# A layernorm's root on 128 columns, two products at a time, and a later front part

## The chip, the cores and the metric

The kernel runs on one core of a Trainium2 chip. Five engines work side by side, each through its own queue of instructions in order: TensorE (PE, matmuls; its weight loads are listed as PEld), VectorE (DVE), ScalarE (ACT), GpSimd (POOL, which here mostly starts DMAs) and SyncE (SP, which starts the other DMAs). The metric is the device time of one execution in microseconds (us), lower is better.

## The reference

The input is 8 images of 256 channels on 32 x 32 places, so 8 batches of 1024 tokens. Two layers follow each other. The first is a state-space block and a small two-layer network, the second is attention and a mixture of experts:

```python
xn = layernorm(x)                                  # over the 256 channels
xm, z = split(xn @ W_in)                           # 512 channels each
xm = silu(conv4(xm) + conv_b)                      # 4 taps along the tokens
dt, Bm, Cm = split(xm @ W_x, [16, 32])             # 16 + 16 + 16 columns
dt = softplus(dt @ W_dt + b_dt)                    # 16 -> 512
h = exp(dt * A) * h + (dt * xm) * Bm               # 16 states for each of 512 channels, in token order
y = (sum over states of h * Cm) + xm * D
x = x + (y * silu(z)) @ W_out
x = x + gelu(layernorm(x) @ W1 + b1) @ W2 + b2
t = x + attention(layernorm(x))                    # 8 heads, 1024 tokens, a bias for each key
xf = layernorm(t)
out = t + layernorm(xf + two chosen experts(xf)) * gamma + beta
```

There are five layernorms over 256 channels on each token: `a` before the state-space block, `f` before the small network, `t` before attention, `x` before the experts, `y` at the end.

## The kernel before

**Tiling.** Channels lie on the 128 partitions, tokens along the free dimension, in chunks of 512 tokens: two chunks for each batch, 16 in all. A 256-channel activation of a chunk is one tile of 128 x 2 x 512 floats. Everything is float32, and a float32 matmul shows as two records in the trace.

**The steps of the scan.** The main loop goes over 16 chunks x 32 steps (`nsteps` = 512). A step is one state of one half of the 512 channels: `inputs` (a product `hb<-xm,bc` on DVE), two calls of `scan` (each a TENSOR_TENSOR_SCAN of 128 x 512 on DVE, fed by an exponential `da` from ACT, made by `decay` two steps ahead), `sums` (a product `hb<-hb,bc` on DVE), after which a DMA that POOL starts adds `hb` into the sum `dx`. In the first chunk of a batch POOL also copies the last column (`state`). bc is loaded two states ahead (`AHEAD`).

**The streams around it.** All other work is written as generators: `prologue(i)` (the front part of chunk i: layernorm, input projection, convolution, dt), `gate_part(i)`, `epilogue(i)` (output projection, small network, layernorm `t`), `attention(b)`, `project_part`, `experts(b)`, `finish`. A planner at build time gives each operation a cost, keeps a planned time for each engine and, between two DVE operations of the scan, takes from each stream what its plan says is ready (`advance`). The order thus written is fixed: on the chip each engine runs its queue in that order and waits where an operand is not there yet. Where the plan finds PE without work it puts in a filler matmul (`keep_warm`: tile `warm`, or zeros added to an open sum of attention).

**What starts when.** `prologue(i + 1)` is started at step `FRONT` = 2 of chunk i, the gate part at step `GATE` = 17, `epilogue(i)` after the last step of chunk i. From step 30 on the scan of a chunk needs the next chunk's `dt`; when the front part has not given it, the planner calls `idle`: DVE gets no scan work there, while the other streams go on. Attention of a batch starts when both epilogues of the batch are done; experts when both chunks of attention are projected.

**Layernorm.** `layernorm` takes the mean by two matmuls with a constant 1/256 matrix (`mu`, 128 x 512), subtracts (DVE), squares (ACT), takes the variance by two such matmuls (`var`, 128 x 512: all 128 rows hold the same numbers), then 1/sqrt by ACT (`Ln`, `Exp`, `Square`, each 128 x 512) and one Newton step on DVE (two operations of 128 x 512), and a last DVE operation scales the tile: one of 128 x 1024, or for `x` and `y` two of 128 x 512. There are 16 of each kind, 80 in all.

**dt.** In the front part, `dbl` (48 rows: 16 for dt, 16 for B, 16 for C) is copied out of PSUM by ACT, one DMA stores the B and C rows (`bc_d`), and four matmuls with 16 rows of `w_dt` give dt for 128 channels each (tile `v`), each in a PSUM bank of its own, read by two ACT operations (`Abs`, `Relu`) before the next is asked for. Softplus goes on with ACT, one DVE operation (`e<-u,e`) and two adding DMAs started by POOL (`dt<-e`, `dt<-u`); the last operation is `xm<-xm,dt` on DVE for each half.

**PSUM.** Eight banks: two single banks (`banks`), two pairs (`pairs`, four banks, attention's scores), and two for attention's sums. A stream may borrow a half of a pair where no bank is free.

Nearly all records carry the line of a recording helper (L100, DMAs started by POOL or SP L95), so the views are read by tile names.

Of the kernel before, what the change touches and what calls it, by code (L numbers as in the profile page):

```python
# [9 lines left out]
F32 = mybir.dt.float32  # L10
BF16 = mybir.dt.bfloat16
I32 = mybir.dt.int32
AF = mybir.ActivationFunctionType
# [41 lines left out]
def hybrid_kernel(ctx: ExitStack, tc: tile.TileContext, a: dict, out: bass.AP):  # L55
# [85 lines left out]
    w_in = load("w_in", [P, KC, 2 * DI], a["W_in"].rearrange("(k p) n -> p k n", p=P))  # L141
    w_x = load("w_x", [P, ND, RK + 2 * NS], a["W_x"].rearrange("(k p) n -> p k n", p=P))
    w_dt = load("w_dt", [RK, DI], a["W_dt"])
    w_out = load("w_out", [P, ND, C], a["W_out"].rearrange("(k p) n -> p k n", p=P))
# [18 lines left out]

    ident = const.tile([P, P], F32, name="ident")
    make_identity(nc, ident)
    mean_c = const.tile([P, 1], F32, name="mean_c")
# [3 lines left out]
    pool.memset(zero_c, 0.0)  # L170
    zero_w = zero_c.to_broadcast([P, P])
    eps_t = const.tile([P, 1], F32, name="eps_t")
    pool.memset(eps_t, EPS)
# [3 lines left out]
    qscale = 1.0 / math.sqrt(HD)  # L177
    neg_a = const.tile([P, ND * NS], F32, name="neg_a")
    act.activation(neg_a, V("A_log"), AF.Exp)
    vec.tensor_scalar(neg_a, neg_a, -1.0, None, ALU.mult)  # L180
# [33 lines left out]
    base2 = const.tile([P, NF], F32, name="base2")  # L214
    gamma2 = const.tile([P, KC], F32, name="gamma2")

# [29 lines left out]
    T4, H4, PT, AHEAD, LAG, TICK = 25, 4, 4, 2, 8.0, 0.15  # L246
    FRONT, GATE = 2, 17

# [62 lines left out]
    class Banks(Slots):  # L311


        lent, halves = {}, []

        def take(self, name):
            while not self.ready() and not (len(pairs.free) == 2 and pairs.ready()):
                yield POLL
            if self.ready():
                return self.now(name)  # L320
            pair = pairs.now(name)
            ps = pair[:, 0, :]
            self.lent[id(ps)] = (ps, pair)
            return ps

        def put(self, ps):
# [41 lines left out]
    def layernorm(tmp, bank, src, dst, name, gain=None, bias=None, sums=None, stored=None):  # L368
# [17 lines left out]
        yield  # L386
        var = yield from bank.take(f"var_{name}")
        for k in range(KC):
            pe.matmul(var, mean_w, sq[:, k, :], start=(k == 0), stop=(k == KC - 1))
        yield  # L390

        r, h = sq[:, 0, :], sq[:, 1, :]
        act.activation(r, var, AF.Ln, bias=eps_t)
# [3 lines left out]
        vec.scalar_tensor_tensor(h, var, EPS, h, ALU.add, ALU.mult)  # L397
        bank.put(var)
        vec.scalar_tensor_tensor(r, h, -3.0, r, ALU.add, ALU.mult)
        if gain is None and sums is None:  # L400
            vec.scalar_tensor_tensor(
                dst, dst, -0.5, r.unsqueeze(1).to_broadcast([P, KC, CH]), ALU.mult, ALU.mult
            )
        else:
            for k in range(KC):
                vec.scalar_tensor_tensor(
                    dst[:, k, :], dst[:, k, :], -0.5 if gain is None else gain[:, k : k + 1], r,
                    ALU.mult, ALU.mult, accum_out=None if sums is None else sums[:, k, :],
                )
                if bias is not None:  # L410
                    vec.tensor_scalar(
                        dst[:, k, :], dst[:, k, :], bias[:, k : k + 1], None, ALU.add
                    )
        tmp.put(sq)
        return dst
# [23 lines left out]
    def prologue(i: int):  # L439
# [52 lines left out]
        for d in range(ND):  # L492
            pe.matmul(
                ps[: RK + 2 * NS, :], w_x[:, d, :], xm[d // 2][:, d % 2, :],
                start=(d == 0), stop=(d == ND - 1),
            )
        yield
        dbl = work_pool.tile([P, KW - 1 + CH], F32, name=f"dbl_{i}", tag="xp", bufs=2)
        dbl = dbl[: RK + 2 * NS, :CH]
        act.copy(dbl, ps[: RK + 2 * NS, :])  # L500
        banks.put(ps)
# [10 lines left out]

        for d in range(ND):
            h, q = divmod(d, 2)
            if q == 0:
                e = yield from mem.take(f"e_{i}_{h}")
                dts.append((yield from mem.take(f"dt_{i}_{h}")))
            ps = yield from banks.take(f"v_{i}_{d}")
            pe.matmul(ps, w_dt[:, d * P : (d + 1) * P], dbl[:RK, :], start=True, stop=True)
            if d == 0:  # L520
                bc_d = dram.tile([NS, 2, CH], F32, name=f"bc_d_{i}", tag="bc_d", bufs=3)
                sp.dma_start(bc_d.rearrange("s g t -> g s t"), dbl[RK:, :])
                me["bc_d"] = bc_d
            yield
            act.activation(e[:, q, :], ps, AF.Abs, bias=V("b_dt", d))
            act.activation(dts[h][:, q, :], ps, AF.Relu, bias=V("b_dt", d))
            banks.put(ps)
            if q == 0:
                continue
            u = yield from mem.take(f"u_{i}_{h}")  # L530
# [218 lines left out]
    def column_bias(pl):  # L749
# [3 lines left out]

        tr = pl.tmp("tr", [P, 4, P], I32)
# [196 lines left out]
    def expert_constants(pl):  # L953
        vec.memset(loads_e, 0.0)
        vec.tensor_scalar(gamma2, V("gamma"), -0.5, None, ALU.mult)
        for dst, n, step, mul, add in (
# [434 lines left out]
    def finish_last(b, c, r, r2, t, xf):  # L1391
# [17 lines left out]
    def finish(b: int, c: int, r, y):  # L1409
# [4 lines left out]
        yield pool.dma_start(out=r, in_=xf_d[b][c], accum_op=ALU.add)  # L1414
        yield from layernorm(mem, banks, r, r, f"y{b}_{c}", gamma2)
        yield
# [9 lines left out]

    def attention_any(pl, b: int):

# [75 lines left out]
    with tc.tile_pool(name="work", bufs=1) as work_pool:  # L1504
# [11 lines left out]
        class Scratch:  # L1516
# [155 lines left out]
    with tc.If(large != 0):  # L1672
        with tc.tile_pool(name="general", bufs=1) as pl:
            wqg = pl.tile([P, KC, NPAIR, P], F32, name="wqg")
            nc.sync.dma_start(wqg, a["Wq"].rearrange("(k p) (j n) -> p k j n", p=P, n=P))
# [14 lines left out]
            for b in range(B):  # L1690
                attention_any(pl, b)


        with tc.tile_pool(name="moe", bufs=1) as pl:
            io = pl.tile([P, E], F32, name="io_e")
            io_i = pl.tile([P, E], I32, name="io_ei")
# [97 lines left out]
            for b in range(B):  # L1794
# [33 lines left out]
                for c in range(NCH):  # L1828
# [13 lines left out]
                    for m in range(KC):  # L1842
# [13 lines left out]
                        r, res,  # L1856
                        f"m{n}", gamma2, V("beta"),
                    ))
# [63 lines left out]
```

## Time and profile before

| | |
|---|---|
| time before, median of 3 runs | 3675.86 us (3664.82, 3675.86, 3676.42) |
| the profiled execution | 3671.49 us, span 3669.6 us |
| mean granted clock of TensorE | 0.953 |
| PE busy (fillers too) | 3313.7 us, 90% |
| DVE busy | 3111.7 us, 85% |
| ACT busy | 2515.7 us, 69% |
| POOL busy | 950.3 us, 26% |
| HBM read and written | 234.36 MB and 58.20 MB, 80 GB/s |
| first scan starts, last scan ends | 92.3 us, 3226.8 us |

How to read the lines: in the page's second part a digit is the busy share of one of 40 equal slices of the span, in tenths. In the stretches each row is a window of the span, then for each engine its busy time and the number of its records. In the groups each row is an engine, an operation, out<-in by tile names, the shape, the count | busy time of all, mean duration of one in ns | idle time of the engine just before them, and what ended it. A matmul's shape begins with rows*columns of the array that it uses. In the timeline a row is start, duration, engine, operation, and in brackets the idle time of the engine just before.

### The profile page before, as it was taken

What the parts mean: (1) busy time and instruction counts of PE and PEld (TensorE: products, weight loads), DVE (VectorE), ACT (ScalarE), POOL (GpSimd) and SP (SyncE); (2) the same over time, 40 slices, a digit from 0 to 9 for tenths busy, and PEclk for the clock granted to TensorE, in tenths of its full rate; (3) what the DMA queues carried; (4) which work ended last, traced back from release to release, by engine and by line L of the source; (5) the groups of instructions that cost most, each with busy time, mean ns of one, the idle gap of its engine ahead of it and who ended that gap; (6) DMA issues with size and microseconds to landing.
All of it is one profiled execution on the core that took longest, in us unless ns stands there. A gap on an engine that the chain in (4) does not pass through costs nothing. (4 is left out here: it accounts for less than half of the span.)

```text
span 3669.6 us, 37029 instructions
## 1 busy us (share of the span) xinstructions
PE 3313.7 (90%) x13023; PEld 1404.1 (38%) x13023; DVE 3111.7 (85%) x3323; ACT 2515.7 (69%) x3437; POOL 950.3 (26%) x1047
## 2 busy tenths in 40 slices
PE   8866869998999998999899999989999989999997
PEld 5553434233343334333433334332433334334333
DVE  5979999999999999999999799999999999942121
ACT  3443746795868776878678877878578876764644
POOL 0323123212431224222322233222423233201010
PEclk9877989999999999999999999999999999999999
DMA  3457777787788778797878877897879887842130
GB/s 110 111 112 177 173 169 167 173 187 180 181 188 189 178 163 197 170 206 180 199 174 193 191 187 171 199 202 160 198 172 201 195 194 181 195 96 69 30 79 14
DMA packets 178868, 597.08 MB, mean 163 GB/s; under 512 B 25184, under 2 KB 27872, under 8 KB 178672
## 3 DMA queue, kind: packets, MB, share of 16 engines
q0 software_dynamic: 103392, 364.44, 50.9%
q1 hardware_dynamic: 75280, 230.18, 19.5%
q8 instruction: 104, 1.70, 0.2%
q14 instruction: 92, 0.75, 0.1%
HBM read 234.36 MB, written 58.20 MB: 80 GB/s over the span
## 5 line engine op out<-in xcount | busy, mean ns | idle before, releaser
L100 ACT ACTIVATE da<-dt,neg_a 128x512 f32<-128x512 f32 x1024 | 718.6, 718 | 525.7 <-DVE hb L100 506.0
L95 POOL DMA_DIRECT2D dx<-hb x512 | 444.2, 868 | 1671.0 <-DVE hb L100 1407.1
L100 DVE TENSOR_TENSOR hb<-hb,bc 128x1024 f32<-128x1024 f32 x512 | 624.5, 1220 | 39.3 <-POOL state L100 25.6
L100 DVE TENSOR_TENSOR_SCAN hb<-da,state,hb 128x512 f32<-128x512 f32 x512 | 631.1, 1267 | 6.0 <-ACT da L100 6.0
L100 DVE TENSOR_TENSOR hb<-xm,bc 128x1024 f32<-128x1024 f32 x512 | 615.9, 1203 | 10.1 <-DMA dx<-hb 10.1
L100 DVE TENSOR_TENSOR_SCAN hb<-da,hb 128x512 f32<-128x512 f32 x512 | 601.9, 1209 | 5.2 <-ACT da L100 5.1
L100 ACT ACTIVATE pt<-sc 128x1024 f32<-128x1024 f32 x512 | 493.5, 1016 | 71.5 <-PE sc L100 68.4
L100 PE MATMUL warm<-mean_c,zero_c 128*128 128x256 f32 x1568 | 440.5, 413 | 46.5 <-DVE x L100 6.5
L100 PEld LDWEIGHTS warm<-mean_c,zero_c 128*128 128x128 f32 x1568 | 293.7, 200 | 216.0 <-PE warm L100 73.9
L100 PE MATMUL sc<-qk,qk 32*128 32x512 f32 x2048 | 337.3, 642 | 19.1 <-ACT pt L100 15.7
L100 POOL COPY state<-hb 128x2 f32<-128x2 f32 x256 | 236.1, 922 | 424.1 <-DVE hb L100 407.7
L100 PE MATMUL num<-pt,v 128*32 128x512 f32 x2048 | 280.9, 618 | 25.1 <-DVE ot L100 24.4
L100 PE MATMUL den<-pt,ecb 128*32 128x512 f32 x2048 | 274.9, 606 | 0.0
L100 PE MATMUL facc<-fh,w 128*128 128x512 f32 x512 | 240.5, 621 | 18.5 <-ACT dt L100 5.9
L100 PE MATMUL fh<-x_f,w 128*128 128x512 f32 x480 | 229.6, 609 | 6.1 <-DVE x_f L100 2.3
L100 ACT ACT_TABLE_LOAD x171 | 219.4, 1283 | 8.5 <-PE var_a L100 4.9
L100 PE MATMUL he<-xe,g 128*128 128x512 f32 x448 | 220.9, 618 | 2.4 <-ACT he L100 2.1
L100 PE MATMUL re<-he,g 128*128 128x512 f32 x472 | 213.9, 598 | 1.2 <-ACT fh L100 0.6
L100 PEld LDWEIGHTS sc<-qk,qk 32*128 32x128 f32 x2048 | 99.3, 183 | 221.5 <-ACT pt L100 86.7
L100 PE MATMUL mo<-sz,w_out 128*128 128x512 f32 x256 | 129.0, 650 | 59.9 <-DVE sz L100 57.1
L100 PEld LDWEIGHTS facc<-fh,w 128*128 128x128 f32 x512 | 98.9, 198 | 152.9 <-issue 125.9
L100 DVE SCALAR_TENSOR_TENSOR xm<-xp,vecs,xm 128x512 f32<-128x512 f32 x192 | 143.4, 747 | 13.5 <-ACT xm L100 9.0
(328 smaller groups left out, 4231.7 us busy)
## 6 DMA issues: line engine op xcount, KB each, us to landing
dx<-hb POOLq DMA_DIRECT2D x512, 512.0 KB
bc<-bc_d SPq DMA_DIRECT2D x256, 512.0 KB
dt<-e POOLq DMA_DIRECT2D x32, 512.0 KB
dt<-u POOLq DMA_DIRECT2D x32, 512.0 KB
xe<-xf_d SPq DMA_DIRECT2D x28, 512.0 KB
xn<-in_x SPq DMA_DIRECT2D x16, 512.0 KB
xn_d<-xn SPq DMA_DIRECT2D x16, 512.0 KB
xz<-xn_d SPq DMA_DIRECT2D x16, 512.0 KB
```

What stands on the lines that cost most here:

```text
L95: f(*args, **kw)
L100: return f(*args, **kw)
```

## The change

Three things are changed, and small ones that follow from them.

1. **dt's products in pairs.** `w_x` has its 16 dt columns twice, in the order dt, B, dt, C, so `dbl` has 64 rows and the dt rows lie at rows 0 to 15 and 32 to 47. `w_dt` is laid out to match. The four matmuls become two pairs; the two of a pair read different rows of the array and write two banks, which are taken together (`take_two`: two single banks, or a whole pair). The four ACT operations on a pair follow together. The B and C rows are stored by two DMAs, since they are no longer neighbours.
2. **Narrow roots.** The variance matmuls write a quarter of the tokens each into 32 rows: eight matmuls (2 halves of the channels x 4 quarters) of 32 columns of the array and 128 tokens, instead of two of 128 x 512. `Ln`, `Exp`, `Square` and the Newton step then work on 128 x 128. Four matmuls with a column of `pick` (zeros, and -0.5 in the first row of a group of 32) spread the four quarters again over all 128 partitions, into the bank that held the variance, and the last DVE operation takes its factor from there. The factor -0.5 is now in `pick`.
3. **`FRONT` = 8**: `prologue(i + 1)` starts at step 8 of chunk i.

The identity matrix for transposes is no longer a constant tile but is made where it is used: in the setup stream, in one of now 9 slots that it borrows, and in the branch for rare inputs, which these inputs don't take. `neg_a` overwrites `A_log` in place, and `gamma2` is gone.

```diff
@@ -139,8 +139,16 @@
     work = ctx.enter_context(ExitStack())
     work.enter_context(tc.manual_schedule(engines=set(ENGINES)))
     w_in = load("w_in", [P, KC, 2 * DI], a["W_in"].rearrange("(k p) n -> p k n", p=P))
-    w_x = load("w_x", [P, ND, RK + 2 * NS], a["W_x"].rearrange("(k p) n -> p k n", p=P))
-    w_dt = load("w_dt", [RK, DI], a["W_dt"])
+
+    w_x = const.tile([P, ND, 4 * RK], F32, name="w_x")
+    w_dt = const.tile([3 * RK, NHALF, P], F32, name="w_dt")
+    wx_v = a["W_x"].rearrange("(k p) n -> p k n", p=P)
+    wdt_v = a["W_dt"].rearrange("r (h q n) -> q r h n", q=2, n=P)
+    loads += [
+        (w_x[:, :, : 2 * RK], wx_v[:, :, : 2 * RK]), (w_x[:, :, 2 * RK : 3 * RK], wx_v[:, :, :RK]),
+        (w_x[:, :, 3 * RK :], wx_v[:, :, 2 * RK :]),
+        (w_dt[:RK], wdt_v[0]), (w_dt[2 * RK :], wdt_v[1]),
+    ]
     w_out = load("w_out", [P, ND, C], a["W_out"].rearrange("(k p) n -> p k n", p=P))
     w1 = load("w1", [P, KC, HID], a["W1"].rearrange("(k p) n -> p k n", p=P))
     w2 = load("w2", [P, HID // P, C], a["W2"].rearrange("(k p) n -> p k n", p=P))
...
@@ -161,22 +169,24 @@
     be = load("be", [P, NH], a["be"].partition_broadcast(P))
     br_p = load("br", [P, E], a["br"].partition_broadcast(P))
 
-    ident = const.tile([P, P], F32, name="ident")
-    make_identity(nc, ident)
     mean_c = const.tile([P, 1], F32, name="mean_c")
     pool.memset(mean_c, 1.0 / C)
     mean_w = mean_c.to_broadcast([P, P])
     zero_c = const.tile([P, 1], F32, name="zero_c")
     pool.memset(zero_c, 0.0)
     zero_w = zero_c.to_broadcast([P, P])
+    pick = const.tile([P, 4], F32, name="pick")
+    pool.memset(pick, 0.0)
+    for q in range(4):
+        pool.memset(pick[HD * q : HD * q + 1, q : q + 1], -0.5)
     eps_t = const.tile([P, 1], F32, name="eps_t")
     pool.memset(eps_t, EPS)
 
 
 
     qscale = 1.0 / math.sqrt(HD)
-    neg_a = const.tile([P, ND * NS], F32, name="neg_a")
-    act.activation(neg_a, V("A_log"), AF.Exp)
+    neg_a = V("A_log")
+    act.activation(neg_a, neg_a, AF.Exp)
     vec.tensor_scalar(neg_a, neg_a, -1.0, None, ALU.mult)
     bq4 = const.tile([P, NG], F32, name="bq4")
     bk4 = const.tile([P, NG], F32, name="bk4")
...
@@ -244,7 +253,7 @@
 
 
     T4, H4, PT, AHEAD, LAG, TICK = 25, 4, 4, 2, 8.0, 0.15
-    FRONT, GATE = 2, 17
+    FRONT, GATE = 8, 17
...
@@ -311,7 +320,7 @@
     class Banks(Slots):
 
 
-        lent, halves = {}, []
+        lent, twos, halves = {}, {}, []
 
         def take(self, name):
             while not self.ready() and not (len(pairs.free) == 2 and pairs.ready()):
...
@@ -323,6 +332,24 @@
             self.lent[id(ps)] = (ps, pair)
             return ps
 
+        def take_two(self, name):
+
+            while True:
+                if len(self.free) > 1 and sorted(self.free)[1][0] <= model.t + 0.3:
+                    return [self.now(f"{name}_{n}") for n in range(2)]
+                if len(pairs.free) == 2 and pairs.ready():
+                    pair = pairs.now(name)
+                    self.twos[id(pair)] = pair
+                    return pair[:, 0, :], pair[:, 1, :], pair
+                yield POLL
+
+        def put_two(self, both):
+            if len(both) == 3:
+                pairs.put(self.twos.pop(id(both[2])))
+            else:
+                for ps in both:
+                    super().put(ps)
+
         def put(self, ps):
             if id(ps) in self.lent:
                 pairs.put(self.lent.pop(id(ps))[1])
...
@@ -384,33 +411,45 @@
             sq = src
         act.activation(sq, dst, AF.Square)
         yield
-        var = yield from bank.take(f"var_{name}")
+
+        ps = yield from bank.take(f"var_{name}")
+        var = ps[:, :P]
         for k in range(KC):
-            pe.matmul(var, mean_w, sq[:, k, :], start=(k == 0), stop=(k == KC - 1))
-        yield
-
-        r, h = sq[:, 0, :], sq[:, 1, :]
+            for q in range(4):
+                pe.matmul(
+                    var[HD * q : HD * q + HD, :], mean_w[:, :HD], sq[:, k, q * P : q * P + P],
+                    start=(k == 0), stop=(k == KC - 1),
+                )
+        yield
+
+        r, h = sq[:, 0, :P], sq[:, 1, :P]
         act.activation(r, var, AF.Ln, bias=eps_t)
         act.activation(r, r, AF.Exp, scale=-0.5)
         act.activation(h, r, AF.Square)
         yield
         vec.scalar_tensor_tensor(h, var, EPS, h, ALU.add, ALU.mult)
-        bank.put(var)
         vec.scalar_tensor_tensor(r, h, -3.0, r, ALU.add, ALU.mult)
+        yield
+
+        for q in range(4):
+            pe.matmul(
+                ps[:, q * P : q * P + P], pick[:, q : q + 1].to_broadcast([P, P]), r,
+                start=True, stop=True,
+            )
+        yield
         if gain is None and sums is None:
-            vec.scalar_tensor_tensor(
-                dst, dst, -0.5, r.unsqueeze(1).to_broadcast([P, KC, CH]), ALU.mult, ALU.mult
-            )
+            vec.tensor_tensor(dst, dst, ps.unsqueeze(1).to_broadcast([P, KC, CH]), ALU.mult)
         else:
             for k in range(KC):
                 vec.scalar_tensor_tensor(
-                    dst[:, k, :], dst[:, k, :], -0.5 if gain is None else gain[:, k : k + 1], r,
+                    dst[:, k, :], dst[:, k, :], 1.0 if gain is None else gain[:, k : k + 1], ps,
                     ALU.mult, ALU.mult, accum_out=None if sums is None else sums[:, k, :],
                 )
                 if bias is not None:
                     vec.tensor_scalar(
                         dst[:, k, :], dst[:, k, :], bias[:, k : k + 1], None, ALU.add
                     )
+        bank.put(ps)
         tmp.put(sq)
         return dst
...
@@ -491,13 +530,13 @@
         ps = yield from banks.take(f"dbl_{i}")
         for d in range(ND):
             pe.matmul(
-                ps[: RK + 2 * NS, :], w_x[:, d, :], xm[d // 2][:, d % 2, :],
+                ps[: 4 * RK, :], w_x[:, d, :], xm[d // 2][:, d % 2, :],
                 start=(d == 0), stop=(d == ND - 1),
             )
         yield
         dbl = work_pool.tile([P, KW - 1 + CH], F32, name=f"dbl_{i}", tag="xp", bufs=2)
-        dbl = dbl[: RK + 2 * NS, :CH]
-        act.copy(dbl, ps[: RK + 2 * NS, :])
+        dbl = dbl[: 4 * RK, :CH]
+        act.copy(dbl, ps[: 4 * RK, :])
         banks.put(ps)
         yield
...
@@ -510,23 +549,25 @@
             landed[h] = pool.dma_start(out=dts[h], in_=t, accum_op=ALU.add)
             mem.put(t, at=landed[h])
 
-        for d in range(ND):
-            h, q = divmod(d, 2)
-            if q == 0:
-                e = yield from mem.take(f"e_{i}_{h}")
-                dts.append((yield from mem.take(f"dt_{i}_{h}")))
-            ps = yield from banks.take(f"v_{i}_{d}")
-            pe.matmul(ps, w_dt[:, d * P : (d + 1) * P], dbl[:RK, :], start=True, stop=True)
-            if d == 0:
+        for h in range(NHALF):
+            e = yield from mem.take(f"e_{i}_{h}")
+            dts.append((yield from mem.take(f"dt_{i}_{h}")))
+            both = yield from banks.take_two(f"v_{i}_{h}")
+            for q, ps in enumerate(both[:2]):
+                rows = slice(2 * RK * q, 2 * RK * q + RK)
+                pe.matmul(ps, w_dt[rows, h, :], dbl[rows, :], start=True, stop=True)
+            if h == 0:
                 bc_d = dram.tile([NS, 2, CH], F32, name=f"bc_d_{i}", tag="bc_d", bufs=3)
-                sp.dma_start(bc_d.rearrange("s g t -> g s t"), dbl[RK:, :])
+                for g in range(2):
+                    rows = slice((2 * g + 1) * RK, (2 * g + 2) * RK)
+                    sp.dma_start(bc_d[:, g, :], dbl[rows, :])
                 me["bc_d"] = bc_d
             yield
-            act.activation(e[:, q, :], ps, AF.Abs, bias=V("b_dt", d))
-            act.activation(dts[h][:, q, :], ps, AF.Relu, bias=V("b_dt", d))
-            banks.put(ps)
-            if q == 0:
-                continue
+            for q, ps in enumerate(both[:2]):
+                d = 2 * h + q
+                act.activation(e[:, q, :], ps, AF.Abs, bias=V("b_dt", d))
+                act.activation(dts[h][:, q, :], ps, AF.Relu, bias=V("b_dt", d))
+            banks.put_two(both)
             u = yield from mem.take(f"u_{i}_{h}")
             act.activation(e, e, AF.Exp, scale=-1.0)
             act.activation(u, e, AF.Identity, bias=1.0)
...
@@ -752,6 +793,8 @@
 
 
 
+        ident = pl.keep(4, "ident", [P, P], F32)
+        make_identity(nc, ident)
 
         tr = pl.tmp("tr", [P, 4, P], I32)
         yield sp.dma_start(tr, a["edge_tgt"].rearrange("(g p) l -> p g l", p=P))
...
@@ -952,7 +995,6 @@
 
     def expert_constants(pl):
         vec.memset(loads_e, 0.0)
-        vec.tensor_scalar(gamma2, V("gamma"), -0.5, None, ALU.mult)
         for dst, n, step, mul, add in (
             (rev_e, E, 1, -1.0, float(E)), (base1, KC, P, 1.0, float(E * C)),
             (base2, NF, P, 1.0, float(E * F)),
...
@@ -1395,7 +1437,7 @@
         vec.tensor_tensor(r, r, xf, ALU.add)
         yield
         mem.put(r2, xf)
-        yield from layernorm(mem, banks, r, r, f"y{b}_{c}", gamma2)
+        yield from layernorm(mem, banks, r, r, f"y{b}_{c}", V("gamma"))
         for m in range(KC):
             vec.scalar_tensor_tensor(
                 r[:, m, :], r[:, m, :], V("beta", m), t[:, m, :], ALU.add, ALU.add
...
@@ -1523,8 +1565,8 @@
                 return work_pool.tile(shape, dtype, name=name, tag=f"t4_{self.slots[n]}")
 
             def tmp(self, name, shape, dtype):
-                self.k = (self.k + 1) % (len(self.slots) - 4)
-                return self.keep(4 + self.k, name, shape, dtype)
+                self.k = (self.k + 1) % (len(self.slots) - 5)
+                return self.keep(5 + self.k, name, shape, dtype)
...
@@ -1583,9 +1625,9 @@
                 yield from attention(b)
 
         def setup():
-            mem = Owner(t4, 8)
+            mem = Owner(t4, 9)
             tiles = []
-            for n in range(8):
+            for n in range(9):
                 tiles.append((yield from mem.take(f"setup_{n}")))
             held = []
             for n in range(2):
```

Left out above: the declaration of `gamma2`, the same replacement of `gamma2` by `gamma` in `finish` and in the branch that is not taken, and the identity matrix in that branch.

More of the change, by code (lines that the diff above doesn't have):

```diff
@@ L214, in hybrid_kernel @@
     base2 = const.tile([P, NF], F32, name="base2")
-    gamma2 = const.tile([P, KC], F32, name="gamma2")
     t_d, xf_d, x1_d = {}, {}, {}
@@ L1414, in finish @@
         yield pool.dma_start(out=r, in_=xf_d[b][c], accum_op=ALU.add)
-        yield from layernorm(mem, banks, r, r, f"y{b}_{c}", gamma2)
+        yield from layernorm(mem, banks, r, r, f"y{b}_{c}", V("gamma"))
         yield
@@ L1425, in gtmp, with attention_any @@
         return Loose(lambda n: pl.tile([P, 2, CH], F32, name=n, tag="t4", bufs=4))
-    def attention_any(pl, b: int):
+    def attention_any(pl, b: int, ident):
         x1 = pl.tile([P, KC, L], F32, name=f"gx1_{b}", tag="x1", bufs=2)
@@ L1673, in hybrid_kernel @@
         with tc.tile_pool(name="general", bufs=1) as pl:
+            ident = pl.tile([P, P], F32, name="ident")
+            make_identity(nc, ident)
             wqg = pl.tile([P, KC, NPAIR, P], F32, name="wqg")
@@ L1690, in hybrid_kernel @@
             for b in range(B):
-                attention_any(pl, b)
+                attention_any(pl, b, ident)
         with tc.tile_pool(name="moe", bufs=1) as pl:
+            ident = pl.tile([P, P], F32, name="ident_e")
+            make_identity(nc, ident)
             io = pl.tile([P, E], F32, name="io_e")
@@ L1856, in hybrid_kernel @@
                         r, res,
-                        f"m{n}", gamma2, V("beta"),
+                        f"m{n}", V("gamma"), V("beta"),
                     ))
```

## Prediction

> **What bounds the kernel now.** I read the page first, then stretches, then the groups with their shapes, then the timeline at the stalls. On the page:
>
> ```profile
> span 3669.6 us, 37029 instructions
> ...
> PE 3313.7 (90%) x13023; PEld 1404.1 (38%) x13023; DVE 3111.7 (85%) x3323; ACT 2515.7 (69%) x3437; POOL 950.3 (26%) x1047
> ...
> DVE  5979999999999999999999799999999999942121
> ```
>
> PE's 90% holds fillers (1568 `warm` records, 440.5 us), DVE's 85% does not: its digit is 9 while the scan runs, from 92.3 to 3226.8, and falls behind it. Two chunks of the scan and the stretch behind it (window, length, busy time by engine):
>
> ```profile
> 1864.80:2069.50 204.70, 197.36 (x823) 70.47 (x822) 184.97 (x175) 169.26 (x227) 44.81 (x49) 0.99 0.79 183
> 2069.50:2272.80 203.30, 190.60 (x709) 78.39 (x712) 193.82 (x219) 151.05 (x211) 74.35 (x81) 0.97 0.81 189
> 3226.80:3669.60 442.80, 414.82 (x1820) 164.40 (x1818) 91.89 (x183) 227.94 (x276) 33.48 (x36) 0.98 0.20 53
> ```
>
> Chunk 10 (second row) is DVE's: 193.8 of 203.3. Chunk 9 is also near PE's limit, 197.4 of 204.7, and DVE stands still in one place, where the next chunk's front part is late:
>
> ```profile
> 2042.14 1.23 DVE L100 TENSOR_TENSOR xm<-xm,dt 128x1024 f32<-128x1024 f32 x1 [4.60 <-DMA dt<-u]
> ...
> 2052.87 1.22 DVE L100 TENSOR_TENSOR re<-re,mu_y 128x1024 f32<-128x1024 f32 x1 [9.50 <-PE mu_y L100]
> ...
> 2054.00 1.22 DVE L100 TENSOR_TENSOR xm<-xm,dt 128x1024 f32<-128x1024 f32 x1
> ```
>
> The last 442.8 us are PE's (414.8). So a microsecond off DVE counts until 3226.8, one off PE counts behind it, ACT is nowhere the limit.
>
> **Root on 128 columns, DVE.** Groups and single tiles:
>
> ```profile
> L100 DVE SCALAR_TENSOR_TENSOR sq_a<-var_a,sq_a 128x512 f32<-128x512 f32 x16 | 10.9, 683 | 12.5 <-ACT sq_a L100 12.3
> L100 DVE SCALAR_TENSOR_TENSOR sq_a<-sq_a 128x512 f32<-128x512 f32 x16 | 11.1, 692 | 0.5
> L100 DVE SCALAR_TENSOR_TENSOR io_ch<-io_ch x1: 291/291/291, 48.3 to 48.3; 128x128 f32<-128x128 f32 x1
> L100 DVE TENSOR_TENSOR b_gm<-b_g,b_blk x4: 281/288/292, 228.5 to 245.5; 128x128 f32<-128x128 f32 x4
> L100 ACT ACTIVATE b_gm<-b_g x4: 277/278/278, 229.7 to 246.7; 128x128 f32<-128x128 f32 x4
> ```
>
> The two Newton operations go from 683 + 692 to 2 x 0.291 (the same operation at that width; 0.288 from PSUM): 0.79 us less for each layernorm. The last one is as long as before: 1.225, against 1.210 for `xn<-xn,mu_a`, which also reads PSUM. By the order of instructions 66 of the 80 layernorms stand between first and last scan, 1 before, 13 behind: 66 x 0.80 = 53 us. In the new order 68 stand there; two more, with some 3.3 us of DVE each, are done before the last scan instead of behind: +6. **DVE: -47.**
>
> From 512 to 128 columns 0.40 of 0.69 goes, not three quarters: (692 - 291) / 384 = 1.04 ns for each column and 0.16 us that stays. [...]
>
> **A new wait.** The last operation of a layernorm now waits for four `pick` matmuls, which wait for Newton's second step; behind it in DVE's queue stand the next scan and product, and all streams that wait for DVE. The nearest rows, in the window 450:3150: operations that wait for `mu` on PE stood idle 33.5 us in 62 layernorms, 0.54 each (many of those start at a DMA's landing); the first Newton step waits for ACT 4.8 us in all, 0.08 each. `pick` follows no DMA, so I take 0.15: 68 x 0.15 = **+10**, between +5 and +37. Below nothing it can't be, since no such wait is taken away.
>
> **PE.** `v` and its nearest relatives:
>
> ```profile
> L100 PE MATMUL sc<-qk,qk 32*128 32x512 f32 x2048 | 337.3, 642 | 19.1 <-ACT pt L100 15.7 <-ACT qk L100 2.2 <-ACT fh L100 0.9
> L100 PE MATMUL v<-dbl,w_dt 16*128 16x512 f32 x128 | 73.4, 661 | 10.6 <-ACT dbl L100 6.5 <-ACT xr L100 2.5 <-DVE sq_y L100 1.0
> L100 PE MATMUL var_a<-sq_a,mean_c 128*128 128x512 f32 x64 | 32.4, 630 | 0.5 <-ACT sq_a L100 0.4
> ```
>
> `v` costs 73.4 / 64 = 1.15 each, alone; `sc`, four row groups at a time, 337.3 / 1024 = 0.33. A pair costs between 0.66 and 2.3; I take 1.05 (two passes of some 0.5), so 73 becomes 34 over the run, 2.4 less for each chunk. The variance was 32.4 / 16 = 2.03 for each layernorm. Its eight narrow matmuls: `den` with four of 32 columns at once has 274.9 / 1024 = 0.27 for 512 tokens, so 8 x 0.07 = 0.5 at best, 0.9 if each group waits for its weights; `pick`, 8 records, is between 0.11 (`logits`, 128x8) and 0.15 (`tt`, 128x128) each: 0.9 to 1.2. And the array changes shape twice more:
>
> ```profile
> 2036.12 1.88 PE L100 MATMUL z<-xz,w_in 128*128 128x512 f32 x4
> 2037.84 1.88 PE L100 MATMUL he<-xe,g 128*128 128x512 f32 x4
> 2039.65 0.71 PE L100 MATMUL sc<-qk,qk 32*128 32x512 f32 x4
> ```
>
> Four records take 1.72 to a neighbour of the same shape and 1.81 to one of another: 0.09 for a change. Sum 1.6 to 2.3, taken as 1.9: even. [...] So PE loses some 40 - 10 us, of which only the few places where DVE waits for PE count: **-4** (-10 to +6).
>
> **FRONT = 8.** Starting later, the front part ends later. In the new order the last `xm<-xm,dt` of the next chunk stands at step 30, the first at which it is needed, in chunks 3, 5, 7, 9, 11 and 13; before in 7, 9, 11 and 13. A place where the scan is held shows as much PE work between two neighbouring scans and little for DVE. Priced by the rows: before, in chunk 9, PE 25.8 and DVE 8.1, so 17.7 too much, of which the timeline above shows 14.1 as idle DVE (0.8), and 9.5 too much in chunk 13, with 2.6 idle seen. After: chunk 7, 26.1 against 8.9; chunk 9, 34.9 against 14.8; chunk 11, 27.5 against 13.4; less 2.3 each for pairs: 44.5, x 0.8 = 36. Against 17 before: **+19**, between -5 (the share of chunk 13) and +28. The moved DMAs (x loads on SP, `dt` adds on POOL) only pass scan DMAs of the same queues; SP issues one more DMA a chunk (0.73 us) and is idle mostly; the next chunk's `bc` is read from step 28, some 50 us behind, so nothing, or 16 x 0.73 = 12 if SP were the late one. POOL's identity and `pick` lie in the 42 us in which it waits for DVE at the start. A pair now holds two banks for four ACT operations of 0.69, 2.8 us; streams that want a bank there can borrow a half of a pair, and the order written already contains that.
>
> **Behind the last scan.** The work put into the held places is missing there. By the order of instructions: `sc` 184 to 169, `num` and `den` 188 to 176 each, the experts' second products 71 to 64, two means and two variances less. By rows: 15 x 0.33 + 24 x 0.27 + 7 x 0.91 + 2 x (2.0 + 2.0) = 26 of PE; but 19 more fillers (0.5 to 0.8) stand there, a sign of waits: **-13**, between 0 and -26. Here 11 layernorms are on or near the path; ACT's three operations fall from 2.0 to 0.83 and DVE's by 0.8, against some 1.5 for `pick` and one more hop: nothing. Before the first scan one layernorm: **-1**. ACT's saving of 80 x 1.1 us elsewhere is covered by DVE.
>
> **Sum.** -47 + 10 - 4 + 19 - 13 - 1 = -36. The profiled execution had 3671.5, between lowest and median of the runs (3664.8, 3675.9): 3636.
>
> **Rivals.** *A: the idle places don't grow, PE's relief gives the front part its time back.* For it: ACT and PE shrink; against it: the held places stand in the order. Then -47 + 5 - 10 - 26 - 1 = -79: 3593; with half of the tail's gain 3606. *B: `pick` waits as `mu` does* (+37) and the tail gains nothing: -47 + 37 + 19 - 4 - 1 = +4: 3675. For it: PE is 95% busy and more in chunks 7 and 9; against it: of `mu`'s 33.5 us 9.5 are the held place above, and about a third follow a DMA. *C, slower: the late front part.* Its four adding DMAs a chunk land later than planned (the DMA share is 0.8), and each of the six odd chunks 3 to 13 is held for 18 us, not three of them for 12: 6 x 18 - 17 = +91, and -47 + 10 - 4 - 26 - 1 = -68: +23, 3694. It decides from 14 us for each of the six on ((68 + 17) / 6). For it: the 14.1 us above; against it: in chunks 3 and 5 little PE work stands at the place. *D: the pairs don't overlap, so the change does not do what it says there:* `v` stays at 73 and the -4 goes, inside the range.
>
> **Numbers.** Forecast 0.60 (own range 3615 to 3660), A 0.17, B 0.10, C 0.13; D changes none. 0.3%, 11 us, is about what a measurement of this kernel tells from no change. Faster 0.77, same 0.10, slower 0.13. The range takes in most of A and B up to its bound, and leaves out C: 3596 to 3674.
>
> **What would show it.** DVE groups of 128x128 near 0.29 with 0.1 to 0.2 idle before the scaling operation, waiting for PE; `v` busy near 34; idle before `xm<-xm,dt` or its neighbours above 30 us in sum, in chunks 7, 9, 11; last scan near 3205 (3227 - 47 + 10 - 4 + 19). Wrong: a wait for `pick` above 0.5, idle at step 30 of chunks 3 and 5, or an unchanged stretch behind the last scan.

## The result and the profile after

The changed kernel takes 3619.07 us (median of 4 runs, 3618.45 to 3622.53) against 3676.14 for the kernel before beside it: a ratio of 0.9853, 95% interval 0.9832 to 0.9874. That is faster, by 57 us where 36 were forecast. The total looks like the forecast's mechanism with some size missing. It is not: one of its three parts did nearly the opposite of what the sum said, and the sum came out near for other reasons. The experiments show this.

The page after, its head and DVE's row of slices:

```profile
span 3617.5 us, 40108 instructions
...
PE 3232.5 (89%) x14487; PEld 1439.5 (40%) x14487; DVE 3039.5 (84%) x3322; ACT 2444.3 (68%) x3437; POOL 949.5 (26%) x1052
...
DVE  4989999999999999989999889989999989941021
```

DVE has 72 us less to do (3111.7 before). The plateau of nines ends earlier, but now has more eights in its second half: part of what DVE saved came back as idle time. First chunks 1 to 15 of the scan as one row, in the kernel before and in the changed kernel (window, length, busy time by engine: PE, PEld, DVE, ACT, POOL):

```profile
323.40:3226.80 2903.40, 2663.03 (x9934) 1078.18 (x9935) 2771.98 (x2789) 2156.12 (x2971) 834.24 (x907) 0.96 0.81 184
311.80:3184.60 2872.80, 2607.36 (x11280) 1103.48 (x11284) 2717.39 (x2801) 2114.70 (x2993) 835.88 (x910) 0.96 0.82 187
```

DVE works 54.6 us less there and is idle 155.4 us instead of 131.4 (length less busy time). Chunk 0 is 12.1 us shorter (219.0 after 231.1), the stretch behind the last scan 9.9, and the first scan starts 0.5 later: together the 52.1 us between the two profiled spans. Then the two chunks and the stretch that the prediction showed, in the changed kernel:

```profile
1824.50:2034.90 210.40, 199.47 (x946) 77.20 (x945) 186.37 (x183) 166.22 (x234) 51.78 (x52) 0.96 0.83 186
2034.90:2230.40 195.50, 176.70 (x715) 76.24 (x713) 183.32 (x210) 140.64 (x202) 67.76 (x76) 0.95 0.80 183
3184.62:3617.50 432.88, 394.07 (x1918) 172.50 (x1918) 76.37 (x173) 200.72 (x254) 30.93 (x33) 0.98 0.18 49
```

Chunk 9 (first row) is 5.7 us longer than before, with only 1.4 more of DVE's work (186.4 of 210.4; 185.0 of 204.7 before); chunk 10 is 7.8 shorter, with 10.5 less. The timeline of DVE ahead of the scans of step 30 of chunk 9 (start, length, instruction, idle before it and its releaser) shows where chunk 9 loses:

```profile
2003.93 1.23 DVE L100 SCALAR_TENSOR_TENSOR e<-u,e 128x1024 f32<-128x1024 f32 x1 [7.03 <-ACT u L100]
...
2010.15 1.41 DVE L100 SCALAR_TENSOR_TENSOR re<-re,vecs,var_y 128x512 f32<-128x512 f32 x2 [2.93 <-PE var_y L100]
...
2015.62 1.23 DVE L100 TENSOR_TENSOR xm<-xm,dt 128x1024 f32<-128x1024 f32 x1 [4.07 <-ACT dx L100]
```

These three waits alone are 14.0 us, between two neighbouring scans, and every one is for a step of the next chunk's front part or of work packed in beside it. Summed from the trace, from the second scan of step 27 to that of step 31 (the "held places" below), DVE's idle time in chunks 1 to 15 grew from 27 to 55 us, 12.9, 16.4 and 14.6 of it in chunks 7, 9 and 11, the three that the prediction named.

The groups of the changed steps:

```profile
L100 DVE SCALAR_TENSOR_TENSOR sq_a<-var_a,sq_a 128x128 f32<-128x128 f32 x16 | 4.3, 271 | 9.5 <-ACT sq_a L100 9.5
L100 DVE SCALAR_TENSOR_TENSOR sq_a<-sq_a 128x128 f32<-128x128 f32 x16 | 4.7, 292 | 0.5
L100 DVE TENSOR_TENSOR tn_t<-tn_t,var_t 128x1024 f32<-128x1024 f32 x15 | 18.2, 1212 | 5.9 <-PE var_t L100 5.6
L100 PE MATMUL var_a<-sq_a,pick 128*128 128x128 f32 x128 | 18.3, 288 | 5.6 <-DVE sq_a L100 5.6
L100 PE MATMUL var_a<-sq_a,mean_c 128*32 128x128 f32 x256 | 10.7, 287 | 1.7 <-ACT sq_a L100 1.3 <-ACT re L100 0.3
L100 PE MATMUL v<-dbl,w_dt 16*128 16x512 f32 x128 | 40.0, 675 | 6.5 <-ACT dbl L100 3.7 <-ACT pt L100 2.3
```

The root's two DVE operations cost 0.271 and 0.292 us where they cost 0.683 and 0.692. The last operation of a layernorm has a wait for PE that it did not have (third row, 5.9 us in the 15 layernorms of that kind). PE's share of a layernorm's root is (18.3 + 10.7) / 16 = 1.81 us, against 2.03. The tile `v` has 128 records in both kernels: 40.0 us hold the pairs where 73.4 held single products.

### The profile page after: what moved, and what is told of

Read it like the earlier page. It is cut to its first block, busy times and chain, and to the rows that moved or that the text cites. A ratio compares the mean times of both kernels' runs of the same rounds, so it can differ in the third digit from the quotient of the medians.

```text
span 3617.5 us, 40108 instructions
## 1 busy us (share of the span) xinstructions
PE 3232.5 (89%) x14487; PEld 1439.5 (40%) x14487; DVE 3039.5 (84%) x3322; ACT 2444.3 (68%) x3437; POOL 949.5 (26%) x1052
## 5 line engine op out<-in xcount | busy, mean ns | idle before, releaser
L100 ACT ACTIVATE da<-dt,vecs 128x512 f32<-128x512 f32 x1024 | 719.2, 718 | 500.3 <-DVE hb L100 488.1
L100 PE MATMUL warm<-mean_c,zero_c 128*128 128x256 f32 x1354 | 394.3, 426 | 44.7 <-ACT dt L100 12.1
L100 PE MATMUL sc<-qk,qk 32*128 32x512 f32 x2048 | 347.8, 649 | 29.9 <-ACT pt L100 24.4
L100 PEld LDWEIGHTS warm<-mean_c,zero_c 128*128 128x128 f32 x1354 | 262.7, 208 | 184.4 <-issue 46.6
L100 PE MATMUL facc<-fh,w 128*128 128x512 f32 x512 | 233.2, 602 | 10.1 <-DVE xf_x L100 7.5
L100 DVE SCALAR_TENSOR_TENSOR xm<-xp,vecs,xm 128x512 f32<-128x512 f32 x192 | 143.5, 748 | 16.0 <-ACT xm L100 11.5
```

What stands on the lines that cost most here:

```text
L100: return f(*args, **kw)
```

## The experiments

The parts can be put in and taken out one by one: **roots** (the narrow layernorm root, with `pick` and the moved identity matrix), **pairs** (dt's products two at a time, `w_x` and `w_dt` widened), **FRONT** (8 or 2). Every kernel below ran beside the kernel before, whose medians lay between 3671.7 and 3674.3.

**e1, FRONT alone.**

```
-    FRONT, GATE = 2, 17          (in the kernel before)
+    FRONT, GATE = 8, 17
```

> Before with FRONT = 8 and nothing else. Theory (DVE's shorter roots bring the gain; a later front part only moves work): DVE busy stays at 3112 us, chunk 0 gets shorter by some 12 us (its waits for the state copies on POOL go), the odd chunks are held more, by 15 to 25 us in all, the stretch behind the last scan gets 5 to 20 us shorter; total 3655 to 3680. Rival (the new order of the work brings the gain, whatever the durations): 3645 or less.

Measured: 3643.22, ratio 0.9927 (0.9905 to 0.9948), the rival's "3645 or less". By itself this part brings 29 us; the prediction had made it a small loss (+19 at the held places, -13 behind the last scan). Here chunks 1 to 15 do get longer, by 19 us against the kernel before (13.5 of it work of DVE that moved in from elsewhere, 5.5 idle time); the gain is the 38 us that the stretch behind the last scan loses (404.9 after 442.8) and 10 in chunk 0:

```profile
313.90:3236.30 2922.40, 2683.41 (x10088) 1077.15 (x10088) 2785.52 (x2811) 2186.14 (x3008) 852.41 (x911) 0.96 0.81 185
```

**e2, pairs alone.**

```
+            both = yield from banks.take_two(f"v_{i}_{h}")      (in the kernel before,
+                pe.matmul(ps, w_dt[rows, h, :], dbl[rows, :], ...)   with w_x and w_dt doubled)
```

> Before with dt's products in pairs and nothing else. Theory: v's busy time on PE 73 to 40 us, DVE busy 3112 as before, and since PE sets the pace in few places 3660 to 3676. Rival (PE's relief brings the gain): 3650 or less.

Measured: 3713.83, ratio 1.012 (1.0103 to 1.0137): slower by 42, outside what was expected, although `v` falls to 39.4 us.

**e3, roots alone.**

```
+                pe.matmul(var[HD * q : HD * q + HD, :], mean_w[:, :HD], ...)   (in the kernel before)
+            pe.matmul(ps[:, q * P : q * P + P], pick[:, q : q + 1]..., r, ...)
```

> Before with the narrow roots (and the identity matrix made in the setup stream) and nothing else. Theory: DVE busy falls by 80 x 0.8 = 64 us to 3048, 68 of these layernorms stand before the last scan, some 13 us come back as waits for pick: 3625 to 3650. Rivals (order, or PE's relief by the pairs): within 10 us of before.

Measured: 3702.19, ratio 1.0077 (1.0058 to 1.0097): slower by 30, outside what was expected, with 67 us less DVE work. The longest waits of DVE in chunks 1 to 15 (sum, times, longest):

```profile
DVE hb L100 <- POOL state L100: 27.1, 7, 6.3
DVE tn_t L100 <- PE mu_t L100: 25.5, 10, 6.4
DVE hb L100 <- ACT da L100: 25.3, 11, 6.0
DVE fo L100 <- ACT fo L100: 20.8, 5, 5.9
```

None of these four is a wait for the factor that `pick` spreads. Those stand under four smaller entries and sum to 25.5 us (the prediction had 10). In all DVE stands idle there for 219 us, against 131 in the kernel before.

**e4, everything but FRONT.**

```
-    FRONT, GATE = 8, 17          (in the changed kernel)
+    FRONT, GATE = 2, 17
```

> The changed kernel with FRONT = 2 again. Theory: a few us from the changed kernel, 3612 to 3640: chunk 0 longer by up to 12, chunks 7, 9 and 11 shorter by 15 to 30 in all, more work behind the last scan. Rival (the order that FRONT = 8 gives brings the gain): 3655 or more.

Measured: 3637.91, ratio 0.9912 (0.9896 to 0.9929), inside what was expected. So FRONT is worth 19 us in this company. The held places stand at 57.7 us with FRONT = 2, against 55.3 with FRONT = 8, and chunks 7, 9 and 11 have 12.8, 15.2 and 10.6 of it: FRONT had not made them.

The parts alone gave -29, +42 and +30, and all three -57. Either the price of a part depends on which others are there, or every new order that the planner writes falls out better or worse by chance. The next four change only the step of the planner's clock, in four of the kernels: the same instructions, in another order.

```
-    T4, H4, PT, AHEAD, LAG, TICK = 25, 4, 4, 2, 8.0, 0.15
+    T4, H4, PT, AHEAD, LAG, TICK = 25, 4, 4, 2, 8.0, 0.16
```

**e5, the kernel before.**

> The kernel before, with the step of the planner's clock at 0.16 instead of 0.15 and nothing else: the same instructions in another order. Theory 'order' (every re-plan scatters the idle time of DVE by tens of us, and that is why the parts alone gave -28, +42 and +30 and all three together -57): DVE's busy time stays at 3111 +- 2, and the time moves by 15 us or more from that of the kernel before, either way, all of it as idle DVE. Rival 'price' (each part has a price of its own that holds in any order): the time stays within 10 us of the kernel before.

Measured: 3699.05, ratio 1.0072 (1.0049 to 1.0095): 25 us slower. Chunks 1 to 15 of this kernel (one row: window, length, PE, PEld, DVE):

```profile
325.70:3260.70 2935.00, 2702.66 (x10068) 1088.77 (x10072) 2780.17 (x2799) 2183.40 (x2993) 836.75 (x911) 0.96 0.80 184
```

DVE's work over the run is 3112.0 us as before, but 154.8 us of this stretch are idle (2935.0 - 2780.2) instead of 131.4.

**e6, the changed kernel.**

> The changed kernel with the planner's step at 0.16. 'Order': DVE's busy time 3040 +- 2, the time 15 us or more away from 3619, more likely above it than below, since 3619 is the best of the orders seen so far. 'Price': 3609 to 3629.

Measured: 3609.86, ratio 0.9822 (0.98 to 0.9843), 9 us faster: inside "price".

**e7, roots alone.**

> Narrow roots alone with the planner's step at 0.16 (alone at 0.15: 3702). 'Order': DVE's busy time 3045 +- 2, and the time comes down by 15 us or more, since 3702 was an unlucky draw; the 64 us that DVE saves show in the time only as an average over orders. 'Price' (single dt products make PE late under narrow roots, in any order): 3692 to 3712.

Measured: 3695.68, ratio 1.0055 (1.0036 to 1.0074): 7 us faster, again "price". Slow roots alone were not one bad draw.

**e8, pairs alone.**

> dt's products in pairs alone with the planner's step at 0.16 (alone at 0.15: 3714). 'Order': DVE's busy time 3112 +- 2, the time 15 us or more away from 3714, likely below it. 'Price' (a pair holds two banks for four ACT operations, and the streams that want a bank are late): 3704 to 3724.

Measured: 3689.16, ratio 1.0042 (1.0027 to 1.0056): 25 us faster, "order".

Two of the four went to each theory, so each holds a part. Spans of the same instructions in two orders lie 24, 16, 15 and 9 us apart; from these four pairs one order of a kernel scatters with a standard deviation of 12 us (the root of the mean square difference, over the root of 2). An attribution by one kernel per part is thus uncertain by more than most parts are worth, and has to be an average over several.

**e9 and e10, the planner's charge for a single dt product**, in roots alone and in the kernel before:

```
+        if op == "matmul" and w.shape[0] == RK:
+            return 1.15          (measured; it charged 0.297)
```

> Narrow roots alone, v one at a time as before, but the planner charges each v product 1.15 us, what it takes, instead of 0.297. Two orders of narrow roots alone took 3702 and 3696, with 219 and 202 us of idle DVE in chunks 1 to 15, against 132 and 155 with wide roots; roots with pairs (FRONT 2) 3638 and 162. Theory 'plan': the single products are charged 6.8 us a chunk too little, PE is late against the plan, and a faster DVE waits for it; pairs are charged 0.30 and take 0.31, so pairs mend the plan. Then the right charge alone brings 3640 to 3670 and idle below 180. Rival 'execution': what DVE lacks is the 33 to 37 us of PE that pairs really take away; then the time stays at 3685 to 3710 and idle at 195 to 225. DVE's busy time 3043 +- 3 by both.

> The kernel before with v charged 1.15 in the plan (two orders of it took 3674 and 3699). If the wrong charge costs time with wide roots as well: 3640 to 3665. If with wide roots DVE is slow enough to cover PE's lateness, within the two orders: 3665 to 3705. DVE's busy time 3111 +- 2.

Measured: e9 3655.58, ratio 0.9948 (0.9932 to 0.9965), with 182 us idle in chunks 1 to 15; e10 3692.37, ratio 1.0061 (1.0038 to 1.0084). The expectation's working was wrong in two places: a chunk has four products, not eight, so the missing charge is 4 x 0.85 = 3.4 us a chunk; and a pair takes 40.0 / 32 = 1.25 us, not twice 0.31. By its time e9 speaks for "plan", by its idle time just not (the profiled execution is its slowest, 3667.1 us); e10 lies between the two orders of the kernel before. The next run takes the ground from "plan".

**e11, the changed kernel without pairs** (roots and FRONT = 8, `v` one at a time, charged 0.297):

```
-            both = yield from banks.take_two(f"v_{i}_{h}")
+            ps = yield from banks.take(f"v_{i}_{d}")
```

> Narrow roots and FRONT = 8 with v one at a time. If the narrow roots need the pairs to show (by 'plan' or by 'execution'): near what the parts alone gave on an average over their two orders, 3686 + 13 - 30 to - 43, so 3655 to 3680, at least 40 slower than the changed kernel. If roots alone had only two unlucky orders: 3610 to 3640.

Measured: 3603.33, ratio 0.9811 (0.9795 to 0.9828), the fastest of all, faster even than the expectation's second case. Roots do not need pairs, and the wrong charge does not have to hurt. Chunks 1 to 15 of this kernel:

```profile
323.80:3169.40 2845.60, 2623.23 (x11196) 1099.76 (x11196) 2719.48 (x2801) 2120.60 (x2995) 841.28 (x911) 0.95 0.84 189
```

DVE works as long as in the changed kernel (2719.5 against 2717.4) and is idle 126.1 us instead of 155.4; the held places are down to 28.

**e12, the changed kernel without roots** (pairs and FRONT = 8, wide root):

```
-        var = ps[:, :P]
+        var = yield from bank.take(f"var_{name}")
```

> Pairs and FRONT = 8 with wide roots. By the parts alone (pairs +15 on an average over two orders, FRONT -30 to -43 in one): 3655 to 3675; if pairs do pay as soon as front parts begin at step 8: 3625 to 3645. DVE's busy time 3111 +- 2.

Measured: 3665.93, ratio 0.9984 (0.9974 to 0.9994), inside the first of the two ranges: without the narrow roots, FRONT = 8 only makes good what pairs alone had cost.

**All eight combinations** are now there. Spans of the profiled executions, the mean of two orders where there are two (e9 and e10 left out, since their planner differs):

| us | wide, FRONT 2 | wide, FRONT 8 | roots, FRONT 2 | roots, FRONT 8 |
|---|---|---|---|---|
| single `v` | 3681.6 (two) | 3641.2 | 3701.2 (two) | 3603.7 |
| pairs | 3702.0 (two) | 3661.6 | 3634.4 | 3613.0 (two) |

The effect of a part is the mean of the four kernels with it less the mean of the four without it, and the same can be done with each stretch. From the scatter of 12 us an effect on the span has a standard error of 7; in the same way it is 0.5 for chunk 0, 2.5 for DVE's work, 8 for its idle time, 4 for the held places and 5 behind the last scan. With medians of the runs in place of the profiled spans the three effects are -35, -3 and -49.

| effect, us | span | chunk 0 | DVE work, chunks 1-15 | idle DVE, chunks 1-15 | of it held places | behind last scan |
|---|---|---|---|---|---|---|
| roots | -33.5 | +1 | -63.0 | +20.1 | +16 | +8 |
| pairs | -4.2 | -3 | 0 | -1 | +6 | +2 |
| FRONT 8 | -50.0 | -8 | +3.5 | -33.8 | -10 | -11.5 |

The three effects add up to -88; from the mean of before's two orders to that of the changed kernel's it is -69. The 19 us between come from one cell of the table, "roots alone": adding the roots is worth -67.6, -37.5 and -48.6 in the other three places, and costs 19.6 there (27 and 12 in its two orders). A mean over the places hides this. FRONT = 8 gains in all four, 40, 40, 98 and 21 us, but the 98 is against that cell; and pairs cost 20, 20 and 9 us in three places and gain 67 in the fourth, again against that cell.

## Why the prediction was right in its total, and where it was not

**DVE, -47, and the wait, +10: right, the wait somewhat small.** The narrow operations cost 0.271 and 0.292, as taken (0.291): at a quarter of the width 0.292 of 0.692 is left, where a quarter of the time would be 0.173. Between the two kernels the durations of DVE's records in chunks 1 to 15, which is what the prediction had priced, fall by 47 in sum; its busy time, in which records that overlap count once, falls by 54.6, and by 63 as the effect over the eight. The +6 for work that one order moves in was no property of the change. The new wait, counted as idle DVE before a layernorm's scaling operation that waits for PE, is 15.5 us in the changed kernel and 17.6 as the effect of the roots, inside the stated +5 to +37 and some 0.25 for each layernorm instead of 0.15. It is there in every kernel with roots (14.8 to 25.8 us); the +20 of idle time beside it is a mean of +67, -11, -4 and +28. With 8 more behind the last scan (standard error 5), where nothing had been forecast, the roots come to -33.5 against -37.

**Pairs, -4: right on PE, not shown in the time.** `v` went to 40.0 instead of 34, since a pair takes 1.25 and not 1.05. The 10 us that the prediction takes off again (40 - 10) no run shows: the roots' own matmuls take 146 us of PE over the run of the changed kernel, against 166 in the kernel before. The 33 us saved on PE moved the span by -4.2 on average, with a standard error of 7, but that this is the forecast's number is luck: it is the mean of +20, +20, +9 and -67. Without the cell "roots alone" pairs only cost time, 17 us on average with a standard error of 8. Of e2's 42 the second order takes away 25 (e8). Whether the rest is a lasting price, of holding two banks for instance, isn't shown.

**FRONT, +19 at the held places: the step that failed.** The prediction took the new order, saw more of PE's work between the scans around step 30 of chunks 7, 9 and 11, and put that down to FRONT. The growth came in those chunks, +28 in all; but e4 has it without FRONT = 8. In the four pairs of kernels FRONT adds 7.5 to the held places at most, and in one pair takes away 48. Even beside the kernel before, where FRONT alone goes with 12 more (e1, 38.9), a mere new order goes with 9 (e5, 35.8). On average the growth follows the roots, by 16 us, though not everywhere (+44, -11, +18 and +13). A likely reason, argued and not shown, is that DVE does each chunk's work some 4 us faster (63 / 15) while PE and ACT still have to bring the next chunk's front part by step 30.

What FRONT does instead was in no step of the sum. The nearest comparison is e4 against the changed kernel, which differ in that number alone; waits of DVE in chunks 1 to 15, of e4 with FRONT = 2:

```profile
DVE hb L100 <- POOL state L100: 26.5, 10, 6.0
DVE hb L100 <- ACT da L100: 19.1, 11, 4.5
DVE xm L100 <- DMA dt<-u: 18.0, 6, 8.2
DVE xf_x L100 <- PE mu_x L100: 12.3, 3, 9.9
DVE tn_t L100 <- PE mu_t L100: 11.9, 8, 2.9
```

and of the changed kernel with FRONT = 8:

```profile
DVE hb L100 <- POOL state L100: 28.8, 7, 6.1
DVE xm L100 <- DMA dt<-u: 13.4, 5, 8.2
...
DVE xf_x L100 <- PE mu_x L100: 7.3, 5, 3.2
...
DVE tn_t L100 <- PE mu_t L100: 5.5, 4, 2.0
...
DVE hb L100 <- ACT da L100: 3.6, 2, 2.2
```

The scan's wait for its own `da` on ACT falls from 19.1 to 3.6. Over all eight combinations the effect of FRONT on that wait is -13 (11 to 25 us in the seven kernels with FRONT = 2, 3 to 8 in the five with FRONT = 8), and on waits for means and variances on PE -15.8. Of the second, 12.6 lies in steps 28 to 31, so that it is for the most part the -10 of the held places once more. As a whole the effect on idle time is uneven: -6, -38, -84 and -7 in the four places.

The load of ACT by itself does not explain the first. In e4 the `da` waits stand, all but 0.2 us, at steps 12 to 19, and with FRONT = 8 ACT does less in steps 4 to 11 (505 against 698 us, durations summed over chunks 1 to 15 and averaged over the combinations) but more in 12 to 23 (1009 against 850), where these waits were. What changes is what stands next to what in ACT's queue. This is ACT before the longest of these waits in e4, 4.5 us in chunk 14:

```profile
2921.60 1.32 ACT L100 ACTIVATE da<-dt,vecs 128x512 f32<-128x512 f32 x2
...
2926.63 3.90 ACT L100 ACTIVATE fh<-fh 128x1024 f32<-128x1024 f32 x4
...
2932.79 0.67 ACT L100 ACTIVATE e<-v,vecs 128x512 f32<-128x512 f32 x1
...
2937.13 2.54 ACT L100 ACTIVATE da<-dt,vecs 128x512 f32<-128x512 f32 x4
```

Between two groups of `da` ACT is busy for 14 us, chiefly with the epilogue's `fh` and, right behind it, the softplus of the next chunk's front part (from `e<-v` on), and the scan waits for the second group. Both stand in the 14 us ahead of each of e4's seven `da` waits over 1 us. With FRONT = 2 the first operations of softplus lie within 14 us of `fh` in 11 to 14 of the 14 chunks that have both; with FRONT = 8 in none to 4, since softplus then comes later (median step 19 or 20 instead of 14 or 15). That the waits go together with this neighbourhood is measured. It does not always make one (the kernel before has it in 14 chunks and three waits over 1 us), and no run moves softplus alone.

Between e4 and the changed kernel DVE's idle time in chunks 1 to 15 falls only by 7 us (162.4 to 155.4), since other waits (`xm` for `xr`, 11.6 in one place) give part of it back. Of the 17 us between their spans 9.5 lie in chunk 0.

**Before the first scan, -1, and chunk 0.** The first scan starts at 92.8 us instead of 92.3. The prediction had no term for chunk 0 itself, and that has 8 us less with FRONT = 8 (standard error 0.5). Its two waits for POOL's `state`, 9.9 us in the kernel before, are not among the longer waits of any kernel with FRONT = 8. The last scan ends at 3184.6 us, where the prediction had 3205.

**Behind the last scan, -13: right for FRONT** on average (-11.5, standard error 5), and 10 us between the two kernels; FRONT alone took 38 away there (e1).

**The rivals.** A (no growth at the held places) and C (all six odd chunks held) are out by the growth in three chunks. B fails by the price of the wait. D is refuted by `v`. What no rival contained is that FRONT takes idle time away inside the chunks, and that the order alone moves the time by 12 us. The forecast of -36 was near by luck, because errors met: -56 in FRONT (-50 instead of +19 - 13 = +6), +4 in the roots (-33.5 instead of -37 and the -1 before the first scan), +19 from the cell "roots alone", and +12 and +5 because the one order of before is 12 faster, and that of the changed kernel 5 slower, than the mean of two. Together: -36 - 56 + 4 + 19 + 12 + 5 = -52, the difference of the two profiled spans.

**What stays open.** Why roots alone are slow in two orders: the charge for `v` helped there (e9) but not with wide roots (e10), and e11 is fast with the wrong charge. It is not TensorE's granted clock: the four executions of e3 had 0.945 on average and those of e11 0.947, and e11 is 99 us faster. And whether pairs cost something beside roots and FRONT: e11 is 7 to 16 us ahead of the two orders of the changed kernel, which the scatter of orders covers. As measured, roots and FRONT without pairs (3603.33) beat both kernels.

## What to carry to other kernels

Where a planner writes the order, measure its scatter first: make a change that leaves every instruction as it is, and treat anything smaller than the difference as unattributed until it is averaged over several combinations. What is saved on the engine that sets the pace can come back in part as its own waiting (here DVE had 54.6 us less to do in chunks 1 to 15 and stood idle 24.0 longer), so look for where it waits next. A mean over several combinations needs a look at its members before it is called a price. And a stall that grows where one forecast it has not been explained until the part that is blamed has been taken out. When the start of a stream is moved, look at what it stood beside in each engine's queue at the place it leaves, not only at what it brings to the place where it ends.

## What the runs showed of the hardware beyond expectation

Two 16-row products issued into two row groups take 1.25 us together (40.0 / 32), against 1.15 for one alone (73.4 / 64): the second costs 0.10. The narrow variance, eight matmuls of 32 columns by 128, takes 10.7 / 16 = 0.67 us for a layernorm where two matmuls of 128 columns by 512 took 2.03 (32.4 / 16). ScalarE at a quarter of the width keeps about half of its time: `sq_a<-sq_a` 631 ns at 128x512, and after:

```profile
L100 ACT ACTIVATE sq_a<-sq_a 128x128 f32<-128x128 f32 x32 | 9.9, 310 | 1.0
```
